# Projecting the values of an attention layer with 64 moving columns per matmul in place of 256

## The chip, the cores and the metric

The kernel runs on one core of a Trainium2 chip. The metric is the device time of one execution in microseconds (us). A core has several engines that run side by side, each with its own instruction stream: TensorE does matrix multiplications (in the profile PE for the matmuls and PEld for the loads of the stationary operand), VectorE (DVE) and ScalarE (ACT) do element-wise work, GpSimd (POOL) does a few element-wise operations, and SyncE (SP) issues most transfers.

## What is computed

Two graph layers over 8 graphs of 2048 nodes with 256 features, each with a residual sum and a layer norm around it. The change lies in the first layer, an attention with 4 heads of 64 features whose softmax runs within chunks of 256 keys:

```python
q = (x @ Wq.T + bq).reshape(B, N, H, Dh).transpose(0, 2, 1, 3)
k = (x @ Wk.T + bk).reshape(B, N, H, Dh).transpose(0, 2, 1, 3)
v = (x @ Wv.T + bv).reshape(B, N, H, Dh).transpose(0, 2, 1, 3)
...
scores = jnp.clip(scores, -10.0, 10.0)
...
attn = jax.nn.softmax(scores, axis=-1)
ctx = jnp.einsum('bhnjc,bhjcd->bhnd', attn, vc)
...
out = ctx @ Wo.T + bo
```

The second layer is a graph attention with its own mask, softmax and weighted mean. All of it is in float32.

## The kernel before

The program is a stream of "beats". There are 512 beats of the first layer: 8 graphs (`b`) times 4 blocks of 512 queries (`ib`) times 8 chunks (`j`) times 2 halves. In a beat TensorE makes the scores of 128 keys against 512 queries for the 4 heads (`sc`, line 948), VectorE clips and masks them (`e`, line 960), ScalarE takes the exponential (line 964), and TensorE multiplies the exponentials of the chunk before by the values and by ones (`u`, line 1016). The second layer of graph `b - 1` is woven into the same beats: VectorE builds scores `w` (lines 805 and 811), ScalarE takes their exponential (line 816), and TensorE adds up the weighted mean (`us`, line 827). Each engine works through its instructions in the order in which the Python code issues them, so the code's order of calls is the order of the work; waits between engines are set by the tile framework.

Most products are made in **quads** (`quads`, line 265 to 269): the 128 output rows are split into four strips of 32, and one matmul is issued for each, with 32 columns of stationary operand and its own quarter of the array's columns. Each program matmul comes with the load of its stationary operand. Because all data is float32, one program matmul appears in the profile as two matmuls with two loads.

The projections use quads too. `proj_T` makes keys and queries with 512 moving columns (`pk`, `pq`). `make_v(b, n)` makes the values of 512 nodes: for each of two result tiles `pv` (128 partitions of 2 x 256 floats, from the pool `ps_m` of two buffers) it takes two strips of 128 nodes (`j`), and for each strip two halves of the contraction (`k`). The stationary operand is the strip of `xt` (128 features by 128 nodes), the moving operand is `WT["v"][:, k, :]` with its 256 columns. ScalarE then copies `pv` to the value tile `v` (line 296). `make_v` is called 32 times, from `projections`, one of the generators that `end_beat` advances; its matmuls therefore stand between the products of one beat and the scores of the next. The output projection of the first layer (`po`) and the one of the second (`pw`) have the same shape as `pv`, 256 moving columns in quads.

Of the kernel before, what the change touches and what calls it, by code (L numbers as in the profile page):

```python
# [19 lines left out]
P = 128  # L20
# [8 lines left out]
def tile_adj_attention__then__gat(  # L29
# [38 lines left out]
    H, D = 4, 64  # L68
    CHUNK = 256
    KC = F // P  # L70
# [37 lines left out]
    def load_w(name, w):  # L108
        t = const.tile([P, KC, F], F32, name=f"WT_{name}")
        nc.sync.dma_start(out=t, in_=w.rearrange("(k p) o -> p k o", p=P))  # L110
        return t
# [11 lines left out]
    WT = {"k": load_w("k", WkT)}  # L123
# [141 lines left out]
    def quads(dst, w, moving, start, stop):  # L265

        for g in range(P // DH):
            r = slice(g * DH, (g + 1) * DH)
            nc.tensor.matmul(dst[r], w[:, r], moving, start=start, stop=stop)  # L269
# [18 lines left out]
    def make_v(b, n):  # L288
        xt = xT_kv.pop((b, n))
        vs[b][n] = one.tile([P, TPB, F], F32, tag=f"v{n}", name=f"v{b}_{n}")  # L290
        for t2 in range(TPB // 2):
            pv = ps_m.tile([P, 2, F], F32, tag="m", name=f"pv{b}_{n}_{t2}")
            for j in range(2):
                for k in range(KC):
                    quads(pv[:, j, :], xt[:, k, ts(2 * t2 + j, P)], WT["v"][:, k, :], k == 0, k == KC - 1)
            nc.scalar.copy(vs[b][n][:, ts(t2, 2), :], pv)

    def projections():


        for b in range(B):
            first = (b * NIB - 1) * 2 * NCH
            for n in range(NIB):


                k_beat = 4 * n - 2 if b == 0 else first + 4 * n + 4
                while beat < k_beat - 2:
                    yield
                if (b, n) not in xT_kv:
                    xT_kv[b, n] = xT_tile(b, n, "k")  # L310
                while beat < k_beat:
                    yield
                if (b, n) != (0, 0):
                    make_kT(b, n)
                    yield
                while beat < k_beat + 2 and b == 0:
                    yield
                make_v(b, n)
# [648 lines left out]
    for J in range(total + 1):  # L967
        b, ib, j = J // (NIB * NCH), J // NCH % NIB, J % NCH
# [158 lines left out]
```

## Time and profile before

| What | Value |
|---|---|
| median of 2 runs | 4084.81 us (4081.47 and 4088.15) |
| profiled execution, its own time | 4088.77 us |
| profiled execution, span from first to last instruction | 4087.0 us |
| VectorE busy | 3199.6 us, 78% of the span |
| ScalarE busy | 2287.0 us, 56% |
| GpSimd busy | 1163.3 us, 28% |
| mean granted TensorE clock | 0.984 of full speed |
| `sc` matmuls, line 948 | x4096, 1031.6 us busy |
| `u` matmuls, line 1016, values and ones | x12288, 984.9 and 497.6 us |
| `us` matmuls, line 827 | x8192, 975.6 us |

A group of the profile holds the instructions of one line with the same tiles and shapes: how many, how long the engine was busy with them (overlaps counted once), and the mean time of one. Matmuls overlap each other in a pipeline, and the four of a quad run side by side, so "busy" divided by the count is much less than the mean time of one. A matmul's end is modelled, its start is recorded.

### The profile page before, as it was taken

How to read it: one execution, taken by the hardware profiler on the slowest of the kernel's cores; microseconds unless marked ns; L12 is line 12 of the kernel's file. 1: busy time of each engine (PE TensorE's matmuls, PEld its weight loads, DVE VectorE, ACT ScalarE, POOL GpSimd, SP SyncE). 2: the span in 40 equal slices, each digit the busy share in tenths (PEclk: the TensorE clock that was granted, in tenths of full speed). 3: DMA queues.
4: the chain of work that ended last, by engine and by line, in shares of the span. 5: the costliest groups of instructions: out<-in, count | busy, mean ns of one | idle time of the engine just before them, and what ended most of it. 6: DMA issues, size and time to landing. Idle time of an engine off the chain costs nothing.

```text
span 4087.0 us, 78798 instructions
## 1 busy us (share of the span) xinstructions
PE 3891.2 (95%) x32796; PEld 1240.8 (30%) x32796; DVE 3199.6 (78%) x5036; ACT 2287.0 (56%) x3238; POOL 1163.3 (28%) x512
## 2 busy tenths in 40 slices
PE   9889999999999999999999999999999999999777
PEld 3222322333233332333223333233323333233222
DVE  5676688679887789868888688877888777887976
ACT  5565555555565565655556555555556555555434
POOL 0232332223333233322233233332333223332300
PEclk9999999999999999999999999999999999999889
DMA  5555433233422333232232323323232232322411
GB/s 164 173 174 156 117 102 93 79 92 100 117 62 82 90 100 107 72 90 82 87 107 83 90 82 98 93 75 101 84 110 77 72 102 89 108 87 82 127 58 58
DMA packets 285541, 400.70 MB, mean 98 GB/s; under 512 B 102239, under 2 KB 153311, under 8 KB 285182
## 3 DMA queue, kind: packets, MB, share of 16 engines
q1 hardware_dynamic: 231168, 361.83, 30.1%
q10 hardware_dynamic: 54014, 33.82, 2.6%
q8 instruction: 257, 4.21, 0.4%
q14 instruction: 102, 0.84, 0.1%
HBM read 340.79 MB, written 52.69 MB: 96 GB/s over the span
## 4 chain that ended last, share of the span: by engine, by line
PE 66%; DVE 21%; DMA 5%; issue 3%; ACT 3%; POOL 1%; ACTq 0%; SPq 0%; DVEq 0%; POOLq 0%
PE u L1016 22%; PE sc L948 16%; PE us L827 15%; DVE e L960 7%; DMA dc<-ds 3%; DVE w L811 3%; PE pk L269 3%; PE po L269 3%; PE pv L269 3%; PE pq L269 3%; PE pw L269 2%; DVE fb L474 2%; DVE w L805 2%; DVE un L1047 1%; DVE dots L408 1%
## 5 line engine op out<-in xcount | busy, mean ns | idle before, releaser
L960 DVE SCALAR_TENSOR_TENSOR e<-sc,mk 128x1024 f32<-128x1024 f32 x1024 | 1203.7, 1216 | 655.9 <-PE sc L948 655.5
L964 ACT ACTIVATE e<-e 128x1024 f32<-128x1024 f32 x1024 | 1076.1, 1056 | 946.5 <-DVE e L960 911.7
L948 PE MATMUL sc<-qT,kT 64*128 64x512 f32 x4096 | 1031.6, 620 | 41.6 <-DVE e L960 38.7
L1048 POOL TENSOR_TENSOR ctxT<-ctxT,un 128x1024 f32<-128x1024 f32 x224 | 535.4, 2390 | 1728.1 <-DVE un L1047 1635.0
L827 PE MATMUL us<-w,hb 128*32 128x512 f32 x8192 | 975.6, 602 | 49.6 <-ACT w L816 45.4
L1016 PE MATMUL u<-e,v 128*32 128x512 f32 x8192 | 984.9, 598 | 4.4 <-ACT ds L1030 4.2
L948 PEld LDWEIGHTS sc<-qT,kT 64*128 64x128 f32 x4096 | 351.0, 186 | 658.1 <-issue 352.4
L1016 PE MATMUL u<-e,ones 128*32 128x512 f32 x4096 | 497.6, 603 | 0.7 <-ACT y L382 0.7
L827 PEld LDWEIGHTS us<-w,hb 128*32 128x32 f32 x8192 | 265.2, 111 | 681.5 <-issue 567.5
L811 DVE SCALAR_TENSOR_TENSOR w<-w,sj,mk 128x512 f32<-128x512 f32 x512 | 457.1, 898 | 5.2 <-DMA mk<-mask 2.5
L805 DVE SCALAR_TENSOR_TENSOR w<-ab,sj 128x512 f32<-128x512 f32 x512 | 439.3, 864 | 25.4 <-DMA ab<-ab_d 19.5
L1016 PEld LDWEIGHTS u<-e,v 128*32 128x32 f32 x8192 | 240.9, 110 | 664.8 <-issue 529.3
L816 ACT ACTIVATE w<-w 128x512 f32<-128x512 f32 x512 | 317.2, 627 | 134.7 <-DVE w L811 68.2
L474 DVE CUSTOM_DVE_ANT_0 fb<-sj_row,fb 128x1024 bf16<-128x1024 f32 x240 | 329.6, 1374 | 19.0 <-issue 15.8
L1024 ACT COPY un<-u 128x512 f32<-128x512 f32 x512 | 296.2, 578 | 80.3 <-PE u L1016 76.1
L1047 DVE TENSOR_TENSOR un<-un,r 128x1024 f32<-128x1024 f32 x224 | 281.3, 1256 | 1.8 <-DMA r<-rd 1.8
L1016 PEld LDWEIGHTS u<-e,ones 128*32 128x32 f32 x4096 | 107.7, 109 | 353.6 <-issue 253.3
L677 POOL TENSOR_TENSOR hx<-hx,hr 128x1024 f32<-128x1024 f32 x28 | 83.7, 2988 | 268.1 <-DVE hx L676 268.1
L1030 ACT COPY ds<-u 128x512 f32<-128x512 f32 x256 | 145.6, 569 | 6.0 <-PE u L1016 6.0
L408 DVE CUSTOM_DVE_ANT_0 dots<-y,wa_bc 128x256 f32<-128x256 f32 x256 | 136.6, 534 | 13.0 <-ACT y L345 0.7
L384 POOL TENSOR_TENSOR y<-y,x 128x1024 f32<-128x1024 f32 x31 | 73.6, 2375 | 239.0 <-ACT y L382 239.0
L269 PE MATMUL pk<-xT_k,WT_k 128*32 128x512 f32 x1024 | 120.8, 614 | 14.2 <-ACT ds L1030 8.6
(112 smaller groups left out, 2405.7 us busy)
## 6 DMA issues: line engine op xcount, KB each, us to landing
r<-rd SPq DMA_DIRECT2D x256, 256.0 KB
mk<-mask SPq DMA_DIRECT2D x120, 512.0 KB
fb<-far SPq DMA_DIRECT2D x240, 256.0 KB
xT_k<-in_xT_dram SPq DMA_DIRECT2D x32, 512.0 KB
raw<-in_adjT_dram SPq DMA_DIRECT2D x32, 512.0 KB
rawf<-in_adj_dram SPq DMA_DIRECT2D x32, 512.0 KB
x<-in_x_dram SPq DMA_DIRECT2D x32, 512.0 KB
h_d<-y ACTq DMA_DIRECT2D x32, 512.0 KB
```

The costliest lines, as they stand in the source:

```text
L269: nc.tensor.matmul(dst[r], w[:, r], moving, start=start, stop=stop)
L474: nc.vector.tensor_tensor_reduce(out=fb, in0=row, in1=fb, scale=1.0, scalar=2 * FAR * 0.999, op0=ALU.add, op1=ALU.max, accum_out=dst,)
L805: nc.vector.scalar_tensor_tensor(self.w, k["ab"][:, 0, :], k["sj"][:, 1, c : c + 1], k["ab"][:, 1, :], ALU.max, ALU.add)
L811: nc.vector.scalar_tensor_tensor(self.w, self.w, k["sj"][:, 0, c : c + 1], k["mks"][c // HT][:, c % HT, :], ALU.add, ALU.min)
L816: nc.scalar.activation(self.w, self.w, AF.Exp)
L827: nc.tensor.matmul(k["us"][g * DH : (g + 1) * DH, n, :], k["hb"][c // TPB][:, c % TPB, f0 : f0 + DH], self.w, start=first, stop=last,)
L948: nc.tensor.matmul(sc[:, h, :], kTs[b][n // TPB][h * D : (h + 1) * D, hp, ts(n % TPB, P)], qTs[b, ib][h * D : (h + 1) * D, hp, :], start=True,
L960: nc.vector.scalar_tensor_tensor(e, sc, -CLIP, cap, ALU.max, ALU.min)
L964: nc.scalar.activation(e, e, AF.Exp)
L1016: nc.tensor.matmul(m[h * DH : (h + 1) * DH, :], prev["v"][pc // TPB][:, pc % TPB, f0 : f0 + DH] if part < 2 else ones[:, 0:DH], prev["es"] ...
L1047: nc.vector.tensor_mul(p["un"], p["un"], r2)
L1048: nc.gpsimd.tensor_add(p["ctxT"], p["ctxT"], p["un"])
```

## The change

In `make_v` the 256 moving columns of a strip are cut into four pieces of 64, one for each head's features. For each piece both halves of the contraction are issued, in quads, so that the same stationary operand is loaded again for each piece. The result tile, its place, its copy and everything else stay as they were.

```diff
             for j in range(2):
-                for k in range(KC):
-                    quads(pv[:, j, :], xt[:, k, ts(2 * t2 + j, P)], WT["v"][:, k, :], k == 0, k == KC - 1)
+                for f in range(H):
+                    for k in range(KC):
+                        quads(
+                            pv[:, j, ts(f, D)],
+                            xt[:, k, ts(2 * t2 + j, P)],
+                            WT["v"][:, k, ts(f, D)],
+                            k == 0,
+                            k == KC - 1,
+                        )
             nc.scalar.copy(vs[b][n][:, ts(t2, 2), :], pv)
```

Here `H` is 4, `D` is 64, `KC` is 2, `P` is 128, and `ts(f, D)` is the slice from `64 f` to `64 f + 64`.

## The prediction, made before the changed kernel had run

> **What bounds the kernel now.** I read the profile's page first: the busy shares, the slices and the chain that ended last.
>
> ```profile
> span 4087.0 us, 78798 instructions
> PE 3891.2 (95%) x32796; PEld 1240.8 (30%) x32796; DVE 3199.6 (78%) x5036; ACT 2287.0 (56%) x3238; POOL 1163.3 (28%) x512
> PE   9889999999999999999999999999999999999777
> ...
> q8 instruction: 257, 4.21, 0.4%
> ...
> PE 66%; DVE 21%; DMA 5%; issue 3%; ACT 3%; POOL 1%; ACTq 0%; SPq 0%; DVEq 0%; POOLq 0%
> PE u L1016 22%; PE sc L948 16%; PE us L827 15%; DVE e L960 7%; DMA dc<-ds 3%; DVE w L811 3%; PE pk L269 3%; PE po L269 3%; PE pv L269 3%; PE pq L269 3%; PE pw L269 2%; DVE fb L474 2%; DVE w L805 2%; DVE un L1047 1%; DVE dots L408 1%
> ```
>
> TensorE is busy 95% of the span and holds two thirds of the chain. `pv` stands in the chain with 3%, some 120 us, which is about all the time it has. So what is added to `pv` should reach the end almost one to one: TensorE's whole idle time is 4087.0 - 3891.2 = 196 us, and only its part that lies soon after a `make_v` could swallow an addition.
>
> Next the groups of TensorE with shapes kept apart, matmuls and then loads (count, busy us, mean ns of one, idle before).
>
> ```profile
> L1016 PE MATMUL u<-e,v 128*32 128x512 f32 x8192 | 984.9, 598 | 4.4 <-ACT ds L1030 4.2
> L269 PE MATMUL pv<-WT_v,xT_k 128*32 128x256 f32 x2048 | 116.6, 379 | 1.6 <-ACT ds L1030 1.4
> L452 PE MATMUL psj<-ident,sj 128*4 128x128 f32 x32 | 8.8, 274 | 16.1 <-DVE sj L408 14.9 <-ACT hx L661 1.2
> ```
>
> ```profile
> L948 PEld LDWEIGHTS sc<-qT,kT 64*128 64x128 f32 x4096 | 351.0, 186 | 658.1 <-issue 352.4 <-DVE e L960 118.0 <-DVE w L805 44.0
> L269 PEld LDWEIGHTS pv<-WT_v,xT_k 128*32 128x32 f32 x2048 | 66.2, 110 | 60.0 <-issue 17.6 <-ACT ds L1030 2.6 <-PE sc L948 0.8
> L452 PEld LDWEIGHTS psj<-ident,sj 128*4 128x4 f32 x32 | 2.6, 81 | 39.9 <-issue 32.1 <-PE us L827 4.4 <-ACT hx L661 1.7
> ```
>
> A matmul of 128, 256 and 512 moving columns takes 274, 379 and 598 ns: (379 - 274) / 128 = 0.82 and (598 - 379) / 256 = 0.86 ns a column, on top of about 170 ns of latency that neighbours share. A load of 4, 32 and 128 columns takes 81, 110 and 186 ns: (186 - 110) / 96 = 0.8 ns a column on top of some 80 ns of latency.
>
> Last, `pv` by itself (minimum, median, maximum ns), and one call of `make_v` in the timeline that follows a wait, first in a short window, then whole (start, time to the end of the last one, count).
>
> ```profile
> L269 PEld LDWEIGHTS pv<-WT_v,xT_k x2048: 106/110/110, 18.1 to 3357.3; 128*32 128x32 f32 x187
> L269 PE MATMUL pv<-WT_v,xT_k x2048: 379/379/403, 18.1 to 3357.5; 128*32 128x256 f32 x187
> ```
>
> ```profile
> 73.88 0.16 PEld L269 LDWEIGHTS pv<-WT_v,xT_k 128*32 128x32 f32 x8 [2.33 <-ACT ds L1030]
> 73.88 0.42 PE L269 MATMUL pv<-WT_v,xT_k 128*32 128x256 f32 x4 [1.42 <-ACT ds L1030]
> ```
>
> ```profile
> 73.88 3.18 PEld L269 LDWEIGHTS pv<-WT_v,xT_k 128*32 128x32 f32 x64 [2.33 <-ACT ds L1030]
> 73.88 3.66 PE L269 MATMUL pv<-WT_v,xT_k 128*32 128x256 f32 x64 [1.42 <-ACT ds L1030]
> ...
> 77.47 0.30 PEld L948 LDWEIGHTS sc<-qT,kT 64*128 64x128 f32 x4 [0.41 <-issue]
> ```
>
> From 73.88 to 77.47 one call issues 64 matmuls, 16 quads, so 3.59 / 16 = 0.224 us a quad, with the first load (403 - 379 = 24 ns) and the turn to `sc` (about 0.1 us) in it. Without these it is (3.59 - 0.024 - 0.1) / 16 = 0.216 us. Streaming 256 columns at 0.84 ns is 214 to 215 ns, so about 2 ns a quad is left as fixed cost. A load of 110 ns lies wholly under 216 ns of streaming: the loads cost nothing today, and this cover is what the change shrinks.
>
> **The change, part by part.** In the two built programs every engine has the same instructions in the same order with the same waits, except that each of the 64 `pv` tiles has 64 program matmuls instead of 16. No transfer is moved, none of the issuing queues changes, and the first matmul of a tile still waits for what it waited for, with the same `sc` queued behind it.
>
> Removed: 512 quads of 256 columns (2048 matmuls and 2048 loads of the profile), 512 x 216 ns = 110.6 us of TensorE. Added: 2048 quads of 64 columns (8192 and 8192).
>
> - *Streaming.* 64 x 0.84 = 53.5 ns, with the 2 ns of fixed cost 55.5 ns; 2048 x 55.5 = 113.7 us, so +3.1 us. With the smaller slope and no fixed cost it is 2048 x 52.5 = 107.5, so -3 us; that is the gain end.
> - *Loads.* A quad now has four times fewer nanoseconds over its loads. Whether a load still fits under 55.5 ns is shown by no row, since no quad streams fewer than 256 columns. Cheap end: the load's own time is its slope, 32 x 0.8 = 26 ns, the rest being latency that is pipelined; then it stays hidden and costs 0. The row for that is the first matmul after a wait, which is only 24 ns longer than the others although its load had just begun. Dear end: a quad cannot follow before the four loads are over, 66.2 us / 512 = 129 ns a set (110 for one), and 2048 x 129 = 264 us, +154 us. I take the cheap end, because the 24 ns row measures just this exposure, in this very product.
> - *Instruction supply.* A quad is 8 engine instructions, one each 55.5 / 8 = 7 ns. Cheap end: after the wait at 73.88, eight loads and four matmuls start within 0.16 - 0.11 = 0.05 us, 4 ns each; cost 0. Dear end: the call above sustains 128 instructions in 3.59 us, 28 ns each, and nothing longer in the trace is denser; 16384 x 28 = 459 us, +349 us. I take the cheap end, since the 28 ns are explained by the streaming alone, but twelve instructions are no proof for 512 in a row.
> - *Copy and result tile.* Same writes, same copy of 0.59 us on ScalarE; 0.
>
> The row of starts bears on a page's rule that speaks against this change. The Trainium skill ("TensorE: Matmul & The Clock Gate", Part 1, "Wait — 56ns, not 53.3ns?") says that matmuls do not start closer together than about 25 ns, however few columns they have. By it, as an estimate, 8192 matmuls take 205 us, +94 us, 4179 us in all. The trace contradicts it within a quad: the four matmuls of the short window, 403 ns each, end within 0.42 us, so they start within 17 ns or so; whether it holds over a long run of quads no row here shows.
>
> Sum: +3.1 us on the profiled execution of 4088.77 us, 4091.9. That execution lies 4.0 us above the median, so 4088 us.
>
> **The rivals.**
>
> *A, streaming sets the pace* (forecast): 4088 us, own range 4078 to 4100 (the -3 us end, and the spread of the runs of 6.7 us). For it: the slopes, the 24 ns and the 4 ns.
>
> *B, a small part shows in each quad.* If the load is never made ahead, each quad pays the 24 ns: 2048 x 24 = 49, with streaming +52 us, 4137 us. Of the same size is the fetch of instructions: queue 8 moved 4.21 MB for 65592 matmuls and loads, 64 bytes each, in 257 packets of 255 instructions, each 0.4% x 16 x 4087 / 257 = 1.0 us long. The 12288 new instructions need 48 more; waited for in full, +49 us. For it: a packet's 256 instructions would be used up in 256 x 7 ns = 1.8 us, hardly longer than the transfer. Against: TensorE's matmuls show no wait of this kind now.
>
> *C, the loads set the pace* (the slower side). A quad can start only when its loads, begun with the quad before, are over with their latency: 110 to 129 ns, 2048 x 110 = 225 or 264 us, less 110.6: +115 to +154 us, 4199 to 4238 us. It decides from the point where a load outlasts the streaming of a quad, some 130 columns. For it: the load's row says 110 ns. Against: the slopes and the 24 ns say that most of it is latency.
>
> *D, the supply of instructions sets the pace* at 28 ns: +349 us, 4434 us. For it: nothing denser is sustained. Against: the dozen at 4 ns.
>
> *E, faster by over 2%.* 82 of the 117 us of `pv` would have to go, with the same columns to stream; I see no way.
>
> **How the numbers follow.** Chances: A 0.47, B 0.18, C 0.20, D 0.13, E 0.02. The time is A's, 4088 us. From 4078 to 4240 the range holds A, B and C, 0.85, and leaves D and E out. About 2%, 82 us, is what a measurement of this kernel can tell from no change; C and D are beyond it: slower 0.20 + 0.13 = 0.33, same 0.47 + 0.18 = 0.65, faster 0.02.
>
> **What would show it.** In the profile after, `pv` should have 8192 matmuls of about 170 + 53 = 223 ns, and one call of `make_v` should still last about 3.6 us until the next `sc`, with `pv` some 120 us busy in all. 5.1 us a call says B's loads, 7 to 8.3 us C, 14 us D; calls of unequal length with gaps in the middle say the fetch of instructions. The idle time before `sc`, `us` and `u` should be as now; if it falls by as much as `pv` grows, the addition was swallowed. The forecast is wrong if loads or supply cannot keep 7 ns an instruction over 512 of them.

## The result, and the profile after

The change costs 2.8%: 4199.08 us median of two runs (4192.89 and 4205.26) against 4084.81, ratio 1.028, 95% interval 1.0205 to 1.0354. The profiled execution took 4205.26 us. The page of the changed kernel, in the lines that were shown of before:

```profile
span 4203.5 us, 91086 instructions
...
PE 3936.1 (94%) x38940; PEld 1310.2 (31%) x38940; DVE 3201.0 (76%) x5036; ACT 2288.0 (54%) x3238; POOL 1162.9 (28%) x512
...
PE   8888999989999999999999999999999999999877
...
q8 instruction: 305, 5.00, 0.5%
...
PE 67%; DVE 20%; DMA 5%; issue 5%; ACT 3%; POOL 1%; ACTq 0%; SPq 0%; DVEq 0%; POOLq 0%
```

12288 instructions were added, and queue 8 moved 48 packets more, as counted beforehand. TensorE's busy time grew by 45 us, and its idle time from 196 to 267 us. "issue", time in which an engine waits for nothing that the profile shows, went from 3% to 5% of the chain. Its groups, shapes kept apart, and then the longest waits of TensorE (total us, times, longest):

```profile
L955 PE MATMUL sc<-qT,kT 64*128 64x512 f32 x4096 | 1047.0, 628 | 41.4 <-DVE e L967 36.8 <-ACT agg L851 2.5 <-issue 1.8
...
L269 PE MATMUL pv<-WT_v,xT_k 128*32 128x64 f32 x8192 | 132.4, 223 | 69.5 <-issue 67.4 <-ACT ds L1037 2.0
L269 PE MATMUL pq<-xT_q,WT_q 128*32 128x512 f32 x992 | 125.1, 638 | 15.2 <-ACT un L1031 10.4 <-issue 2.9 <-ACT hx L668 0.9
```

```profile
PE pv L269 <- issue: 67.4, 27, 4.9
PE us L834 <- ACT w L823: 47.2, 22, 10.9
```

Three things stand there. `pv` itself is busy for 132.4 us, 16 more than before. Before `pv`, TensorE now sits idle 27 times, for up to 4.9 us, with no semaphore to wait for. And `sc` and `pq`, which the change does not touch, are slower (628 for 620 ns, 638 for 607). One call of `make_v` shows all three, in the timeline of TensorE and in a row of stretches around it (length, busy us of PE, PEld, DVE, ACT and POOL, clock, DMA share, GB/s):

```profile
872.83 3.40 PE L269 MATMUL pv<-WT_v,xT_k 128*32 128x64 f32 x227
880.95 0.96 PE L269 MATMUL pv<-WT_v,xT_k 128*32 128x64 f32 x27 [4.72 <-issue]
```

```profile
873.00:876.00 3.00, 3.00 (x228) 3.00 (x218) 1.73 (x2) 0.59 (x1) 1.12 (x1) 1.00 0.48 141
876.00:880.00 4.00, 0.23 (x15) 0.07 (x4) 0.00 (x0) 0.00 (x0) 1.25 (x1) 0.82 0.94 250
880.00:884.00 4.00, 3.05 (x41) 1.81 (x44) 0.00 (x0) 1.93 (x4) 0.00 (x0) 0.50 0.13 46
884.00:888.00 4.00, 4.00 (x28) 1.69 (x22) 0.00 (x0) 2.07 (x5) 0.00 (x0) 0.83 0.32 131
```

227 of the call's 256 matmuls run without a pause, (3.40 - 0.22) / 227 = 14.0 ns each, 56 ns a quad: the pace of streaming. Then TensorE stands still for 4.72 us; in the 4 us that the row from 876 shows, the DMA engines are 94% busy. When it goes on, its granted clock is 0.50 for 4 us.

The difference of the two spans, 116.5 us, comes together like this. Idle by "issue" before `pv` (67.4) and before `pq`, `sc` and `po` (2.9 + 1.8 + 0.9) is 73 us; each of these 30 gaps is some 0.2 us longer than shown, because the last matmul before it is drawn until its modelled end, so about 79. Streaming: 3. The clock: 0.976 of full speed against 0.984 is 4203.5 x 0.024 - 4087.0 x 0.016 = 35 us, an upper bound, as part of it falls into idle time; `sc`, `pq` and `u` are busy 29 us longer for the same work. 79 + 3 + 35 = 117, closer to 116.5 than an upper bound promises. The term of the clock has support beyond this call: in this trace each of the 11 gaps by "issue" of 3.48 us or more is followed by a mean clock of 0.50 to 0.66 over the next 4 us, each of the 12 of 1.74 us or less by 1.00; the seven between them lie on both sides (0.57 to 1.00).

### The profile page after: what moved, and what is told of

Its sections match the earlier page's. It is cut to its first block, busy times and chain, and to the rows that moved or that the text cites. A ratio compares the mean times of both kernels' runs of the same rounds, so it can differ in the third digit from the quotient of the medians.

```text
span 4203.5 us, 91086 instructions
## 1 busy us (share of the span) xinstructions
PE 3936.1 (94%) x38940; PEld 1310.2 (31%) x38940; DVE 3201.0 (76%) x5036; ACT 2288.0 (54%) x3238; POOL 1162.9 (28%) x512
## 4 chain that ended last, share of the span: by engine, by line
PE 67%; DVE 20%; DMA 5%; issue 5%; ACT 3%; POOL 1%; ACTq 0%; SPq 0%; DVEq 0%; POOLq 0%
PE u L1023 22%; PE sc L955 17%; PE us L834 14%; DVE e L967 6%; DMA dc<-ds 4%; PE pv L269 3%; PE pq L269 3%; DVE w L818 3%; PE pk L269 3%; PE po L269 3%; PE pw L269 2%; DVE fb L481 2%; DVE w L812 2%; DVE un L1054 1%; DVE dots L415 1%
## 5 line engine op out<-in xcount | busy, mean ns | idle before, releaser
L955 PE MATMUL sc<-qT,kT 64*128 64x512 f32 x4096 | 1047.0, 628 | 41.4 <-DVE e L967 36.8
L269 PE MATMUL pv<-WT_v,xT_k 128*32 128x64 f32 x8192 | 132.4, 223 | 69.5 <-issue 67.4
L269 PEld LDWEIGHTS pv<-WT_v,xT_k 128*32 128x32 f32 x8192 | 125.8, 112 | 88.5 <-issue 84.2
```

Source lines behind the costliest of these rows:

```text
L955: nc.tensor.matmul(sc[:, h, :], kTs[b][n // TPB][h * D : (h + 1) * D, hp, ts(n % TPB, P)], qTs[b, ib][h * D : (h + 1) * D, hp, :], start=True,
```

## The experiments

Theory F: TensorE runs out of instructions. By the theory they arrive in blocks of 256, a block is asked for when the one before it is begun, and where 256 instructions are used up in 1.8 us the next block is not there yet. Rivals: L, each added matmul and load has its price wherever it stands; C, the loads set the pace, as in the prediction.

**Pieces of 128 columns** (`q128`), half the instructions in the same stretch of time:

```diff
-                for f in range(H):
+                for f in range(F // 128):
                     for k in range(KC):
...
-                            pv[:, j, ts(f, D)],
+                            pv[:, j, ts(f, 128)],
```

> Pieces of 128 columns: 256 instructions a call in place of 512, half as dense (a quad of 8 instructions streams 128 columns, some 109 ns). Theory F (TensorE runs out of instructions where a block of 256 is used up faster than the next is fetched, 3.5 us or more after the block before was begun): a block lasts 256 x 13.7 = 3.5 us even if it lies wholly in a call, so hardly a stall; +2 us of streaming and at most 15 us of stalls, ratio 1.000 to 1.004. Theory L (each added load and matmul has its price wherever it stands; 12288 added cost 114 us): 4096 added, +38 us, ratio 1.009. Theory C of the prediction (a quad takes 110 ns because of its loads): 1024 quads at 110 ns, +2 us.

Measured: ratio 1.0005 (0.9995 to 1.0015). No wait of `pv` by "issue" is left in the trace. L asked for 1.009 and falls; F and C are not told apart by it.

**One strip a beat** (`strips64`), the same 64-column quads, spread out:

```diff
-                make_v(b, n)
+                if b == 0:
+                    make_v(b, n)
+                    continue
...
+                for t in range(TPB):
+                    v_strip(b, n, t, xt)
+                    if t < TPB - 1:
+                        yield
+                    if t == 0 and n + 1 < NIB:
+                        xT_kv[b, n + 1] = xT_tile(b, n + 1, "k")
```

Each strip has a tile and a copy of its own here, and the next block of `x` is fetched after the first strip.

> 64 columns as in the change, but for graphs 1 to 7 each call is cut into its four strips of 128 nodes, one strip a beat with a tile and a copy of its own; graph 0 stays as in the change. Same matmuls and loads, in stretches of 128 instructions. F: with other products between the strips a block of 256 lasts 7 us, so the 25 stalls of graphs 1 to 7 go; left are those of graph 0 (10.7 us in the trace of the change, some 15 with the lower clock behind them) and 3 us of streaming: +15 to +25 us, ratio 1.004 to 1.006. L and C: the same price as in the change, +114 us, ratio 1.028.

Measured: ratio 1.0035 (1.0022 to 1.0048), +14 us, a little under what F gave. The same number of loads and matmuls of the same shape cost nearly nothing, so L and C are out. Four gaps are left, as this line of TensorE's waits says, and all lie in graph 0, which kept its whole calls:

```profile
PE pv L269 <- issue: 9.4, 4, 5.0
```

The four strips of a later call in the timeline of TensorE, each of 64 matmuls, run through:

```profile
876.07 1.08 PE L269 MATMUL pv<-WT_v,xT_k 128*32 128x64 f32 x64
...
882.45 1.08 PE L269 MATMUL pv<-WT_v,xT_k 128*32 128x64 f32 x64
...
890.75 1.08 PE L269 MATMUL pv<-WT_v,xT_k 128*32 128x64 f32 x64
...
900.57 1.08 PE L269 MATMUL pv<-WT_v,xT_k 128*32 128x64 f32 x64
```

**Pieces of 32 columns** (`q32`), the suspected cost made larger. The edit is that of `q128` with 32 in place of 128.

> Pieces of 32 columns: 1024 instructions a call, four blocks of 256, streaming 4096 quads of some 29 ns = 119 us (+8 us). F: each block of a call waits for its fetch, 3.5 us or more, so a call lasts 12 to 18 us with some three stalls of 3 us, and the lower clock comes on top: +330 to +480 us, ratio 1.08 to 1.12; the stalls stand every 256 instructions. L: 28672 added instructions at 114 us for 12288, +266 us, ratio 1.065, without gaps. C: 4096 quads at 110 ns, +340 us, without gaps: a quad follows a quad every 110 ns.

Measured: ratio 1.093 (1.0896 to 1.0963), +381 us, inside F's range and outside L's; C's 340 us is near, but C wants an even pace. The waits and one call in the timeline:

```profile
PE pv L269 <- issue: 236.3, 94, 6.3
```

```profile
2012.34 1.94 PE L269 MATMUL pv<-WT_v,xT_k 128*32 128x32 f32 x128 [2.56 <-issue]
2016.36 1.94 PE L269 MATMUL pv<-WT_v,xT_k 128*32 128x32 f32 x128 [2.08 <-issue]
2020.10 1.19 PE L269 MATMUL pv<-WT_v,xT_k 128*32 128x32 f32 x72 [1.81 <-issue]
```

94 gaps in 32 calls, about three a call, and between two gaps just 128 matmuls, with their loads 256 instructions. From block to block it is 4.02 and 3.74 us. This is the mark of F: the gaps are tied to a count of instructions, not to a tile, a strip or a load. All 62 pairs of neighbouring gaps within a call have exactly 128 matmuls between them, 3.45 us apart at the least. The stretches above ran at a granted clock of 0.50; one at 1.00 is

```profile
491.43 1.28 PE L269 MATMUL pv<-WT_v,xT_k 128*32 128x32 f32 x128 [2.44 <-issue]
```

With 0.19 us for the last matmul's own time, (1.28 - 0.19) / 127 = 8.6 ns a matmul, 4.3 ns an instruction with the loads. So instructions that have arrived are taken faster than the change needs them.

The traces tie the gaps to the packets of queue 8 themselves, whose starts and lengths they hold. In the change's gap of 4.72 us, from 876.23 to 880.95, this line of its DMA queues counts one (packets, MB, share of the 16 engines' time):

```profile
q8 instruction: 1, 0.02, 1.6%
```

It starts at 878.23, lasts 1.24 us, and 1.48 us after its end TensorE goes on. So it is everywhere: the 30 gaps by "issue" in the change end 1.26 to 1.65 us after the end of such a packet, the 94 of `q32` 1.07 to 1.60 us after. In the change's trace, by the medians, the next packet starts 1.15 us after TensorE has gone on, as F says of the block that is asked for when the one before is begun, lasts 1.11, and TensorE, where it stands still for it, goes on 1.40 us after its end: 3.7 us from block to block, against 1.8 us in which a dense block is used up.

**Two neighbouring beats** (`halves64`), stretches of 256 instructions:

```diff
-                make_v(b, n)
...
+                v_half(b, n, 0, xt)
+                yield
+                v_half(b, n, 1, xt)
```

> 64 columns as in the change, but in graphs 1 to 7 the two tiles of a call are made in two neighbouring beats: stretches of 256 instructions, between the 512 of the change and the 128 of strips64. F: a block that holds x instructions of the stretch lasts 0.007x + 0.052(256 - x) us, so only where x is over some 185 (fetch beside other transfers) to 220 (fetch alone) is there a stall, of about 1 to 1.6 us: some 30 us of stalls, 15 of graph 0, 3 of streaming: +35 to +60 us, ratio 1.009 to 1.015, between strips64 and the change. A price for each instruction or load: 1.028 as in the change.

Measured: ratio 1.0043 (1.0028 to 1.0059), +18 us, half of what F had said at least. In graphs 1 to 7 no gap before `pv` is left, only one of 0.9 us before `u`; the four before `pv`, 10.3 us, all lie in graph 0, which kept its whole calls. The formula left something out. A possible reason, which no run tests: if instructions are read some way ahead of the engine, the next block is asked for while the slow instructions before the stretch still run, and these give it time.

**Contention, less of it** (`later64`, with the control `later256`, the kernel before in the same way). In the call above SyncE issues a row of transfers during the call:

```profile
872.57 0.53 SPq L1047 DMA_DIRECT2D r<-rd  x1
...
873.20 0.43 SPq L120 DMA_DIRECT2D xT_k<-in_xT_dram  x1
...
873.68 0.47 SPq L373 DMA_DIRECT2D x<-in_x_dram  x1
874.24 0.48 SPq L546 DMA_DIRECT2D fb<-far  x1
```

That is 1.25 MB behind the 256 KB of `r`. The edit moves the call away from it:

```diff
-                while beat < k_beat + 2 and b == 0:
+                while beat < k_beat + 2:
                     yield
                 make_v(b, n)
```

> 64 columns as in the change, make_v one beat later in graphs 1 to 7, a beat in which no row of transfers begins. F with contention (a block's packet waits behind the transfers that SyncE issues just then, which makes stalls of 4 to 5 us out of stalls of 2): 25 stalls of some 2 us, little lower clock, +3 of streaming and 15 of graph 0: +50 to +75 us, ratio 1.012 to 1.018. F without contention, or L, or C: +114 us as in the change.

> Control: the kernel before (256 columns) with make_v one beat later in graphs 1 to 7. All theories: ratio 1.000, within 0.003; what it differs by is the price of the later place itself and is taken off later64.

Measured: 1.0218 (1.0197 to 1.0238), and 1.0011 (1.0001 to 1.0020) for the control. Less than the change, but not as little as expected: 30 gaps are left, 57.5 us of idle time before `pv`, and the longest is still 5.0 us. The later place does not always clear the way: by the trace, four of the 28 calls of graphs 1 to 7 meet another row of transfers there (`fb`, `xT_q`, `xT_k`), and their gaps are 2.5 to 5.0 us. Of the other 24, two have no gap, 21 have one of 0.8 to 2.0 us, and one has 4.95 us, which stays unexplained.

**Contention, more of it** (`more64`, with the control `more256`):

```diff
+                if b:
+                    nc.sync.dma_start(
+                        out=more_d[b, n], in_=xT[b, :, ts(n, IB)].rearrange("(k p) n -> p k n", p=P)
+                    )
                 make_v(b, n)
```

> The change, with one more transfer for each call of make_v in graphs 1 to 7: SyncE copies the 512 KB of that call's block of x to a spare place in device memory, at the place in its order where the call stands. F with contention: the block's packet waits behind these 1 MB of reading and writing too, so stalls of 1 to 2 us become 3 to 5 and the long ones longer: 28 calls by some 2 to 4 us, with the lower clock behind them +60 to +130 us over the change, ratio 1.043 to 1.060 against the kernel before. F without contention: as the change, 1.028, but for what the control costs.

> Control: the kernel before with the same extra transfer. With 256 columns no block is used up before the next is there, so all theories: ratio 1.000 to 1.003; what it differs by is the price of the transfer itself and is taken off more64.

Measured: 1.0332 (1.0314 to 1.0349), and 0.9997 (0.9987 to 1.0006) for the control. More than the change, but by about a third of the least that was expected. The idle time before `pv` is 76.4 us, and the longest gap 4.8, no longer than in the change. By "issue" before any matmul, each of the three traces has 30 gaps: 57.5 us in all in `later64`, 73.0 in the change, 83.8 here.

**The change once more** (`again64`, no edit), as the measure for these two:

> The change itself once more, in more rounds, so that later64 and more64 can be set against it: ratio 1.028 by the first measurement (1.0205 to 1.0354). F with contention wants it above later64 (1.0218 less 0.0011 of its control) and below more64 (1.0332); F without contention wants all three alike.

Measured: 1.0281 (1.0265 to 1.0297). The three intervals do not touch, so transfers that SyncE issues beside a dense stretch lengthen the gaps: about 0.0281 - (0.0218 - 0.0011) = 0.0074, 30 us, is taken away by the later place, and 0.0332 + 0.0003 - 0.0281 = 0.0054, 22 us, is added by the further copy. The packets show where the time goes. In the change's trace a packet of instructions lasts 0.88 to 1.70 us, and it is its start that comes late: after 23 of the 30 gaps the next one starts within 1.25 us, with the DMA engines at most 39% busy with other packets over the first 1.1 us. After the other seven it takes 1.4 to 5.0 us, and in five of these the engines are over 90% busy with others. Why no gap before `pv` of the 64-column kernels is longer than some 5 us is open.

**A whole load for each 64 columns** (`full64`): the loads' own price, with as few instructions as before.

```diff
-                        quads(
+                        nc.tensor.matmul(
...
-                            k == 0,
-                            k == KC - 1,
+                            start=(k == 0),
+                            stop=(k == KC - 1),
```

> 64 columns, but each piece is one matmul with 128 stationary columns in place of a quad of four with 32: 64 instructions a tile, as before the change, and a load of 128 columns for each. F: no stall, since the stream is no denser than before; a load of 128 columns takes 0.83 x 128 = 107 ns against 54 ns of streaming, and 2048 matmuls follow each other every 107 to 110 ns, 219 to 225 us, +108 to +115 us, ratio 1.027, with an even pitch. If loads cost nothing: +3 us. If a load's whole recorded 186 ns counted: 2048 x 186 = 381, +270 us.

Measured: ratio 1.0322 (1.0273 to 1.0372), +133 us, with no gap by "issue" before `pv`. The group of `pv`, and `pv` in a window inside one call:

```profile
L296 PE MATMUL pv<-WT_v,xT_k 128*128 128x64 f32 x2048 | 235.5, 276 | 1.4 <-ACT ds L1037 1.4
```

```profile
L296 PE MATMUL pv<-WT_v,xT_k x38: 275/275/275, 17.8 to 21.9; 128*128 128x64 f32 x38
L296 PEld LDWEIGHTS pv<-WT_v,xT_k x38: 192/192/192, 17.8 to 22.0; 128*128 128x128 f32 x38
```

38 matmuls from 17.8 to 21.9 are 0.111 us each, a little over the 107 that the slope of the loads gave. So a load of 128 columns does set the pace under 64 moving columns, by its slope and not by its recorded 192 ns. By this pitch 2048 x 111 - 110.6 = +117 us. The profiled execution has that: its span is 4206.1 us against 4087.0 of the kernel before, +119. The median is higher, +133, by the other execution, 4221.41 us at a clock of 0.981; with only two executions this was not followed up.

## Why the prediction was right or wrong, point by point

- **What bounds the kernel**: right. TensorE holds 67% of the chain after as well, and what stopped it reached the end.
- **Streaming, +3.1 us**: right. A quad of 64 columns takes 56 ns for the 55.5 predicted, the matmul 219 to 223 ns for 223, and nothing but the gaps stands between the quads.
- **Loads, cheap end**: right. The slope counts and the latency does not; the 24 ns of rival B's first half do not appear in the run of quads either. `full64` bears the slope out from the other side.
- **Instruction supply, cheap end**: this is the step that failed. It was posed as a rate, 4 ns against 28 ns an instruction. The rate holds at 7 ns over 227 matmuls and their loads, in `q32` even at 4.3 ns, and rival D with its 28 ns falls. But the supply is not a steady flow; it is a block of 256 that is there or is not, and one call of 512 instructions outruns it. The term that the forecast put at nothing measured about 79 us of standstill and up to 35 us of lower clock behind it.
- **The forecast, A**: wrong. The measured median lies 111 us above its 4088 us and 99 us above the end of its own range, 4100.
- **Rival B**: the right mechanism in its second half, and the wrong size. It priced each of the 48 new packets by the 1.0 us of its transfer, 49 us. The transfer was sized rightly, 1.11 us by the median of 305 packets; what B left out is the 1.15 us before it and the 1.40 us after it, so that a block follows a block after 3.7 to 4.0 us in the two intervals of `q32` that the timeline shows, with up to 5 us of standstill where other transfers are in the way: about 79 us in the trace of the change. The further 35 us at most, the lower clock behind the gaps, were in no case of the prediction.
- **Rival C**: its 4199 us agree with the measured median to the microsecond, by chance. In the run of 227 matmuls a quad takes 56 ns, not 110, and `strips64` has all of C's loads at +14 us.
- **The range and the sign**: the range, 4078 to 4240, held the time, but by C's price, which was the wrong reason. "Slower", at 0.33, came true; "same" had 0.65.
- **What would show it**: calls of unequal length with gaps in the middle were named there as the sign of the instruction fetch, and that is what the trace shows.

## What to carry to other kernels

Where a matmul is cut into smaller ones, compare the time in which TensorE uses up 256 instructions (loads count too) with the time in which the next 256 arrive, here 3.5 to 4 us, and more beside other transfers. 512 instructions, which TensorE would take in 3.6 us, cost 2.8%; the same instructions in stretches of 128 or 256 among longer ones cost 0.4%, with 9 to 10 us of gaps in the calls of graph 0 that were left whole, and 256 in about 3.6 us (`q128`) cost nothing that could be measured. Look for idle time put down to "issue" on the engine that bounds the kernel, and add the time after it at a lower clock.

## What the runs showed of the hardware that was not expected

- TensorE can start a float32 quad of 64 columns every 56 ns, matmul after matmul at 14 ns, and one of 32 columns every 34 ns at full clock (`q32`), with the loads beside the matmuls. The Trainium skill ("TensorE: Matmul & The Clock Gate", Part 1, "Wait — 56ns, not 53.3ns?") has a floor of about 25 ns; for matmuls in different column groups these 227 in a row, and the 128 in a row at 8.6 ns, contradict it.
- The fetch of instructions is hidden at 256 instructions in 3.6 us (`q128`) and shows where 512 follow each other at 256 in 1.8 us. The Trainium skill ("Runtime: NRT & Kernel Launch", "Instruction fetch mechanics") says that blocks of 256 instructions are fetched while the one before is executed, which the gaps every 256 instructions fit, and that crossing a block is mostly hidden. That agrees with the kernel before, which has no wait of TensorE by "issue", and not with dense stretches: `q32` stands still 94 times, 236 us in all.
- A packet of instructions can start up to 5 us after TensorE has gone on, in place of 1.1 us, where the kernel's own transfers keep the DMA engines over 90% busy: one copy of 512 KB beside each call of graphs 1 to 7, free in the kernel before (0.9997), costs half a per cent here.
- After a gap of 4.7 us TensorE's granted clock is 0.50 for the next 4 us, and after all 11 gaps of 3.48 us or more it is 0.50 to 0.66, so that a long gap costs more than its length.
